# Where attention values are normalised: per unit on VectorE, or once per token tile on GpSimd

## The chip, the cores and the metric

The program runs on one core of a Trainium2 chip. The metric is the device time of one execution in microseconds (us). The engines are named as in the profile: PE is TensorE's matrix multiplication and PEld its weight load, DVE is VectorE, ACT is ScalarE, POOL is GpSimd and SP is SyncE, which here issues the DMAs.

## The reference

Four batch elements of 512 tokens by 512 channels pass through two layers. The second layer's cross-attention is where the change is:

```python
x = x + tanh(g_xattn[0]) * wkv(layernorm(x), ctx)          # a scan over the tokens
x = x + tanh(g_ffn[0])  * bitlinear_ffn(layernorm(x))      # 512 -> 2048 -> 512, int8 groups
x = x + tanh(g_xattn[1]) * attention(layernorm(x), ctx)
x = x + tanh(g_ffn[1])  * ternary_linear(layernorm(x))

# attention: 16 heads of 32 channels, queries from x, keys and values from ctx
attn = softmax(einsum('bnhd,bmhd->bhnm', q, k) * scale)
o    = einsum('bhnm,bmhd->bnhd', attn, v)
out  = qdq(o) @ qdq(wp).T + bp                             # qdq: int8, one scale per token
```

## The kernel before

A batch element `b` goes through four generators in turn: `wkv_layer`, `ffn_layer`, `attention_layer` and `ternary_layer`. Neighbouring elements overlap: while element `b` is in attention, element `b+1` is in its FFN and element `b+2` or `b+3` in its scan. Each generator is a list of small steps, and `line(gen, parts)` gives the steps a place on a common axis, measured in slots of an FFN; `run` takes them in order of place. The Tile framework's scheduler then settles the order of instructions on each engine, from that order and from what is ready, so that a change in one layer moves instructions of others. Each engine works through its own queue in order.

The attention of one element is cut into 16 units: eight pairs of heads `p`, each for two halves `h` of the tokens (two token tiles of 128). A unit goes through these steps:

- `scores` (line 948 and 950 of the kernel before): PE forms the scores `s_ps`, DVE takes the negated maximum of each row (`at_nm`), and ACT takes the exponential into `at_P`. ACT's accumulator puts the row's sum into the unit's small tile `at_sum`.
- `turned` (line 970): PE turns `at_P` into `pt_ps`, and ACT copies it to `at_PT`.
- `values` (line 990): PE multiplies by the values into `o_ps`, and ACT copies it to `at_os`, 128x128. It is unnormalised and has channels on the partitions.
- `collect` (lines 998 and 1000): PE turns it back into `ot_ps`, DVE takes the reciprocal `at_rt` of the unit's four sums, and DVE multiplies `ot_ps` by it into the unit's place in `o_all` (tile `at_o`, tokens on the partitions, one copy of it).

After the 16 units, `project_out(t)` runs for each of the four token tiles. DVE takes the largest magnitude of the 512 channels (line 222, `at_s` from `at_o`), ACT rounds (line 231), PE turns (`qr_ps`), ACT copies (line 238), PE multiplies by the output weights (`p_ps`), DVE scales (line 1036, `at_y`), and the result is added to `xb` (line 1037, on GpSimd for the first two elements). `in_steps` starts the four tiles one step after the other. The ternary layer follows: layer normalisation, `tf_xn` on GpSimd and `tf_s` on DVE.

The last element (`alone`) has no FFN beside it and takes another path through `turned` and the ending. PSUM tiles of `o_ps`, `ot_ps`, `qr_ps`, `p_ps` and others share three buffers with the tag `m`; score and FFN tiles share three with the tag `hp`.

Other names that the prediction uses: `wk_*` are tiles of the scan of the next element (its reciprocals at line 640, products at lines 632 and 645 on DVE, 630 and 635 on GpSimd). `ff_hp`, `ff_z`, `qg_*` and `hr` belong to the FFN.

Of the kernel before, what the change touches and what calls it, by code (L numbers as in the profile page):

```python
# [10 lines left out]
F32 = mybir.dt.float32  # L11
# [5 lines left out]
ALU = mybir.AluOpType  # L17
# [4 lines left out]
P = 128  # L22
# [8 lines left out]
def kernel(  # L31
# [36 lines left out]
    nc = tc.nc  # L68
    NB, T, D = x.shape
    FF = w1.shape[0]  # L70
    NT, NC, NF = T // P, D // P, FF // D
    NH, DH = 16, 32
# [8 lines left out]
    sm = ctx.enter_context(tc.tile_pool(name="small", bufs=4))  # L81
# [45 lines left out]
    def psum_tile(name, tag, dtype=F32):  # L127
        pool, bufs = psum["now"]
        return pool.tile([P, D], dtype, name=name, tag=tag, bufs=bufs[tag])

    def bank(name, dtype=F32):

        return psum_tile(name, "m", dtype)
# [13 lines left out]
    def in_turn(ins):  # L147


        if "on" in turn:  # L150
            if "ahead" in turn:
                behind(ins, turn["ahead"])
            turn["last"] = ins
        return ins
# [6 lines left out]
    def matmul(*args, **kwargs):  # L161
        return in_turn(nc.tensor.matmul(*args, **kwargs))  # L162

    def transpose(*args):
        return in_turn(nc.tensor.transpose(*args))  # L165
# [55 lines left out]
    def absmax(dst, src):  # L221
        nc.vector.tensor_reduce(dst, src, AX.X, ALU.max, apply_absolute_value=True)

    def int8_scale(s, r, amax):

        nc.vector.tensor_scalar(s, amax, 1.0 / 127.0, 1e-8, ALU.mult, ALU.max)
        nc.vector.reciprocal(r, s)

    def rounded(src, r):

        nc.scalar.activation(src, src, AF.Identity, bias=magic[:, 0:1], scale=r)

    def transposed_rows(dst, src):

        pt = bank("qr_ps")
        for c in range(NC):
            transpose(pt[:, c * P : (c + 1) * P], src[:, c * P : (c + 1) * P], ident)
        nc.scalar.activation(dst, blocks(pt), AF.Identity, bias=magic[:, 1:2])
# [599 lines left out]
    whole = {}  # L838

    def attention_layer(b, xb, pool, tiles=range(NT)):  # L840
# [5 lines left out]
        lo, n = tiles[0] * P, len(tiles) * P  # L846
        alone = b == NB - 1
        if b not in whole:
            whole[b] = (
                pool.tile([P, NC, T], BF16, name="at_xqT", tag="at_xqT", bufs=1),  # L850
                pool.tile([P, T], F32, name="at_sxb", tag="at_sxb", bufs=1),
                pool.tile([P, NT, D], F32, name="at_o", tag="at_o", bufs=1),
            )
        xqT, sxb, o_all = whole[b]

        def row(name, dtype=F32):
            return pool.tile([P, D], dtype, name=name, tag="at_row", bufs=ROWS)
# [24 lines left out]
        qR, kR, V, PT, sums, made, lanes, out_s = {}, {}, {}, {}, {}, {}, {}, {}  # L882
# [54 lines left out]
        def scores(k, i, t):  # L937

            p, h = units[k]
            if k not in sums:  # L940
                sums[k] = sm.tile([P, 2, 2], F32, name="at_sum", tag="at_sum")
            at = t * P
            sp = psum_tile("s_ps", "hp")
            matmul(
                sp, lhsT=qR[k][:, i, at : at + P], rhs=kR[p][:, i, :], start=True, stop=True
            )
            nm = sm.tile([P, 1], F32, name="at_nm", tag="at_nm", bufs=8)
            nc.vector.tensor_reduce(nm, sp, AX.X, ALU.max, negate=True)  # L948
            lanes[k, i, t] = pool.tile([P, T], F32, name="at_P", tag="at_P", bufs=6)
            nc.scalar.activation(  # L950
                lanes[k, i, t],
                sp,
                AF.Exp,
                bias=nm,
                accum_out=sums[k][:, t, i : i + 1],
            )
# [35 lines left out]
        def collect(k):  # L992

            p, h = units[k]
            pt = bank("ot_ps")[:, 0:P]
            transpose(pt, out_s.pop(k), ident)
            rt = sm.tile([P, 2, 2], F32, name="at_rt", tag="at_rt")
            nc.vector.reciprocal(rt, sums.pop(k))
            at = tiles[0] + 2 * h
            nc.vector.tensor_tensor(  # L1000
                o_all[:, at : at + 2, p * 64 : p * 64 + 64].rearrange(
                    "p t (i d) -> p t i d", d=DH
                ),
                pt.rearrange("p (i t d) -> p t i d", i=2, d=DH),
                rt.unsqueeze(3).to_broadcast([P, 2, 2, DH]),
                ALU.mult,
            )
# [9 lines left out]
        def project_out(t):  # L1017
            s = sm.tile([P, 2], F32, name="at_s", tag="at_s")
            o = o_all[:, t, :]
            absmax(s[:, 0:1], o)  # L1020
            int8_scale(s[:, 0:1], s[:, 1:2], s[:, 0:1])
            rounded(o, s[:, 1:2])
            yield True
            oqT = pool.tile([P, NC, P], BF16, name="at_oqT", tag="at_oqT")
            transposed_rows(oqT, o)
            yield True
            pp = bank("p_ps")
            for c in range(NC):
                matmul(
                    pp, lhsT=oqT[:, c, :], rhs=wpT[:, c, :], start=(c == 0), stop=(c == NC - 1)  # L1030
                )
            if b > NB - 3:
                y = wk.tile([P, D], F32, name="at_y", tag="wk_v")
            else:
                y = row("at_y")
            nc.vector.scalar_tensor_tensor(y, pp, s[:, 0:1], swp_b, ALU.mult, ALU.mult)
            (nc.vector if b > NB - 3 else nc.gpsimd).tensor_tensor(
                xb[:, t, :], xb[:, t, :], y, ALU.add
            )
            yield True  # L1040
# [9 lines left out]
        def end(ts):  # L1050

            yield from together([project_out(t) for t in ts])
            means, scale = statistics(b, xb, ts)
            yield from together([ternary(b, xb, pool, t, means, scale) for t in ts])
# [7 lines left out]
        for k in range(len(units) + 2):  # L1062
# [3 lines left out]
            for i in range(2):  # L1066
                if now:
                    scores(k, i, 0)
# [13 lines left out]
            for i in range(2):  # L1082
                if now:
                    scores(k, i, 1)
# [5 lines left out]
            if k > 1:  # L1090
                collect(k - 2)
            if now:
                p, h = units[k]
# [12 lines left out]
        if alone:  # L1106
            yield from ending
        else:
            yield from in_steps([project_out(t) for t in tiles], 1)
# [66 lines left out]
    def ternary_layer(b, xb, pool):  # L1176
        if b == NB - 2:
            r, scale = statistics(b, xb, range(NT))
            yield
        else:  # L1180
            r, scale = layernorm(xb, rms=True, pinned=False), None
        yield from in_steps([ternary(b, xb, pool, t, r, scale) for t in range(NT)], 1)
# [9 lines left out]
    def late(make):  # L1192
        yield from make()
# [26 lines left out]
    SLOTS = NT * NF + 1  # L1220

    def line(gen, *parts, aside=False):
        lines.append({"gen": gen, "parts": parts, "step": 0, "aside": aside})
# [124 lines left out]
    for b in range(NB):  # L1348
        if b:
            early = (0.99, 1.0, 4) if b == 1 else (b - 0.19, b - 0.1, 3), (b - 0.08, b, 1)  # L1350
            line(
                late(lambda b=b: ffn_layer(xs[b])),
                *((early[0],) if b == 1 else early),
                (b, b + 16 / SLOTS, 64),
                (b + 16 / SLOTS, b + 17.75 / SLOTS, 7),
            )
        start = b + 1 + 4.95 / SLOTS
        end = start + 18 / SLOTS
        line(
            late(lambda b=b: attention_layer(b, xs[b], at)),  # L1360
            (b + 1.0 if b == 0 else b + 0.7, b + 1.03 if b == 0 else b + 0.9, 5),
            (b + 1 + 1.7 / SLOTS, b + 1 + 3.7 / SLOTS, 5),
            (b + 1 + 3.75 / SLOTS, b + 1 + 4.35 / SLOTS, 2),
            (start, end, 72),
            (end, end + 2.4 / SLOTS, 6)
            if b != NB - 2
            else (end - 0.15 / SLOTS, end + 4.65 / SLOTS, 6),
            (end + 2.4 / SLOTS, end + 3.4 / SLOTS, 4),
        )
        if b < NB - 1:  # L1370
            line(
                late(lambda b=b: ternary_layer(b, xs[b], at)),
                (end + 3 / SLOTS, end + 8 / SLOTS, 8)
                if b < NB - 2
                else (end + 4.85 / SLOTS, end + 11.85 / SLOTS, 7),
                aside=b < NB - 2,
            )
# [46 lines left out]
```

## Time and profile before

| | |
|---|---|
| median of 3 runs | 1095.68 us (1094.95 to 1096.86) |
| the profiled execution's own time | 1094.21 us |
| its span, first to last instruction | 1092.4 us |
| mean granted TensorE clock | 0.956 |
| busy: PE, DVE, ACT, POOL | 86%, 76%, 67%, 29% |
| share of the chain that ended last: PE, DVE, ACT, POOL | 49%, 22%, 14%, 5% |

The span lies 1.8 us below the profiled execution's time, and the median of the runs 1.5 us above it. The shares of busy time are means over stages with different limits: while a scan runs beside attention and FFN, DVE is full; between the scans PE is.

### The profile page before, as it was taken

To read this page: it belongs to the slowest core of one execution; us is meant where nothing else is said; L and a number is where in the kernel's file an instruction comes from. 1 tells how busy PE (TensorE), PEld (TensorE's weight loads), DVE (VectorE), ACT (ScalarE), POOL (GpSimd) and SP (SyncE) were. 2 spreads that over 40 slices of the span, in tenths; PEclk is the share of its full clock that TensorE was granted. 3 is DMA by queue.
4 is the path that set the end of the run, shared out by engine and by line. 5 is a ranking of instruction groups with operands and counts; after the bars stand their busy time and mean duration, and the time that the engine had idled before them with its cause. 6 is when DMAs were issued, how large, how long until landed. Compare 5 with 4: busy or idle time off the path is not lost.

```text
span 1092.4 us, 17928 instructions
## 1 busy us (share of the span) xinstructions
PE 943.3 (86%) x6350; PEld 680.0 (62%) x6380; DVE 827.0 (76%) x1600; ACT 729.9 (67%) x1490; POOL 320.7 (29%) x328
## 2 busy tenths in 40 slices
PE   3879997998879888799997886999999999878975
PEld 2345564565557666677775665677776777655652
DVE  5985548757876899896769898966687866579976
ACT  5656755567545776667877576677685777877863
POOL 3831104423333254621215545412122410100000
PEclk8889999999999999999999798999999999989998
DMA  8188845464445674645576354655574563244311
GB/s 288 39 272 317 323 169 190 144 221 155 154 146 181 221 234 127 231 129 169 185 234 204 121 177 133 204 195 180 184 231 156 184 210 116 59 148 116 116 42 39
DMA packets 85674, 189.68 MB, mean 174 GB/s; under 512 B 12241, under 2 KB 36817, under 8 KB 74577
## 3 DMA queue, kind: packets, MB, share of 16 engines
q1 hardware_dynamic: 85584, 188.53, 51.7%
q8 instruction: 51, 0.84, 0.3%
q14 instruction: 39, 0.31, 0.1%
HBM read 148.65 MB, written 39.85 MB: 173 GB/s over the span
## 4 chain that ended last, share of the span: by engine, by line
PE 49%; DVE 22%; ACT 14%; POOL 5%; issue 5%; DMA 4%; SPq 1%; ACTq 0%; POOLq 0%; DVEq 0%
PE ff_hp L162 15%; PE pt_ps L165 7%; PE ff_acc L162 6%; PE o_ps L162 4%; PE v_ps L162 4%; PE s_ps L162 3%; ACT at_P L950 3%; DVE wk_q L640 3%; ACT at_PT L970 3%; DVE at_nm L948 2%; PE k_ps L162 2%; DVE wk_p L634 1%; PE qr_ps L165 1%; PE tp_ps L165 1%; ACT wk_e L612 1%
## 5 line engine op out<-in xcount | busy, mean ns | idle before, releaser
L162 PE MATMUL ff_hp<-wT,xp 128*128 128x512 f32 x1024 | 275.7, 412 | 6.6 <-DVE ff_z L746 3.7
L162 PEld LDWEIGHTS ff_hp<-wT,xp 128*128 128x128 f32 x1024 | 195.4, 196 | 54.6 <-DVE ff_z L746 5.7
L950 ACT ACTIVATE at_P<-s_ps,at_nm 128x512 f32<-128x512 f32 x256 | 175.0, 690 | 45.2 <-DVE at_nm L948 43.4
L948 DVE TENSOR_REDUCE at_nm<-s_ps 128x1 f32<-128x512 f32 x256 | 166.6, 677 | 38.4 <-PE s_ps L162 37.9
L970 ACT COPY at_PT<-pt_ps 128x512 f32<-128x512 f32 x224 | 131.2, 590 | 72.6 <-PE pt_ps L165 71.9
L685 POOL TENSOR_TENSOR ff_z<-qg_b,qg_s 128x512 f32<-128x512 bf16 x64 | 71.9, 1124 | 314.6 <-ACT qg_b L684 304.7
L165 PE MATMUL pt_ps<-ident,at_P 128*128 128x128 f32 x1024 | 155.4, 280 | 9.0 <-ACT at_PT L970 4.3
L165 PEld LDWEIGHTS pt_ps<-ident,at_P 128*128 128x128 f32 x1024 | 118.1, 142 | 47.3 <-ACT at_PT L970 10.9
L162 PE MATMUL ff_acc<-wT,hr 128*128 128x512 f32 x512 | 137.6, 409 | 5.2 <-DVE hr L697 2.6
L162 PE MATMUL s_ps<-at_kR,at_qR 128*128 128x512 f32 x256 | 103.0, 464 | 24.0 <-ACT at_P L950 17.6
L162 PEld LDWEIGHTS ff_acc<-wT,hr 128*128 128x128 f32 x512 | 92.9, 191 | 26.2 <-DVE hr L697 4.2
L162 PE MATMUL o_ps<-at_PT,at_V 128*32 128x128 f32 x2048 | 75.4, 281 | 4.7 <-ACT at_PT L970 2.8
L162 PEld LDWEIGHTS o_ps<-at_PT,at_V 128*32 128x32 f32 x2048 | 54.8, 111 | 28.6 <-issue 11.6
L746 DVE SCALAR_TENSOR_TENSOR ff_z<-ff_z,ff_hp 128x512 f32<-128x512 f32 x64 | 43.4, 679 | 37.0 <-ACT ff_z L745 36.9
L745 ACT ACTIVATE ff_z<-ff_hp,coef 128x512 f32<-128x512 f32 x64 | 44.1, 688 | 40.5 <-PE ff_hp L162 38.1
L750 DVE SCALAR_TENSOR_TENSOR ff_z<-ff_hp,coef,ff_z 128x512 f32<-128x512 f32 x64 | 47.7, 745 | 30.2 <-PE ff_hp L162 30.1
L684 ACT CAST qg_b<-qg_i 128x512 bf16<-128x512 int8 x80 | 49.3, 617 | 27.4 <-DVE qg_i L680 17.3
L162 PEld LDWEIGHTS s_ps<-at_kR,at_qR 128*128 128x128 f32 x256 | 43.3, 194 | 36.4 <-ACT at_P L950 25.2
L162 PE MATMUL v_ps<-wkvT,cT 128*128 128x512 f32 x128 | 60.5, 618 | 5.5 <-DVE wT L303 2.3
L162 PE MATMUL k_ps<-cT,wkvT 128*128 128x512 f32 x128 | 61.3, 631 | 2.3 <-ACT wk_k L584 1.0
L640 DVE RECIPROCAL wk_q<-wk_q 128x256 f32<-128x256 f32 x32 | 54.5, 1722 | 3.0 <-POOL wk_q L635 1.6
L696 ACT CAST hr<-tp_ps 128x512 fp32r<-128x512 f32 x64 | 37.6, 588 | 21.7 <-PE tp_ps L165 21.7
(180 smaller groups left out, 1669.4 us busy)
## 6 DMA issues: line engine op xcount, KB each, us to landing
wT<-wD SPq DMA_DIRECT2D x72, 1024.0 KB, 5.4
wn<-in_L_ffn_w_dram SPq DMA_DIRECT2D x18, 1024.0 KB, 6.2
at_kR<-kD SPq DMA_DIRECT2D x128, 128.0 KB, 4.0
at_qR<-qD SPq DMA_DIRECT2D x256, 64.0 KB, 2.5
wD<-wT SPq DMA_DIRECT2D x12, 1024.0 KB, 4.2
kD<-k_half SPq DMA_DIRECT2D x16, 512.0 KB, 2.8
qD<-at_half SPq DMA_DIRECT2D x32, 256.0 KB, 2.2
cn<-in_ctx_dram SPq DMA_DIRECT2D x8, 512.0 KB, 5.9
```

The source lines that it names most:

```text
L162: return in_turn(nc.tensor.matmul(*args, **kwargs))
L165: return in_turn(nc.tensor.transpose(*args))
L640: nc.vector.reciprocal(half, half)
L684: nc.scalar.copy(qb, qi)
L685: nc.gpsimd.tensor_tensor(grouped(src), grouped(qb), s.unsqueeze(2).to_broadcast([P, NG, GS]), ALU.mult)
L696: nc.scalar.copy(part[:, 0, :], pt)
L745: nc.scalar.activation(z, hp, AF.Tanh, scale=coef[:, 0:1])
L746: nc.vector.scalar_tensor_tensor(z, z, 1.0, hp, ALU.add, ALU.mult)
L750: nc.vector.scalar_tensor_tensor(z, hp, coef[:, 1:2], z, ALU.mult, ALU.mult)
L948: nc.vector.tensor_reduce(nm, sp, AX.X, ALU.max, negate=True)
L950: nc.scalar.activation(lanes[k, i, t], sp, AF.Exp, bias=nm, accum_out=sums[k][:, t, i : i + 1],)
L970: made[k] = nc.scalar.copy(dst, blocks(pt))
```

## The change

In the first three elements, `collect` has no arithmetic any more: ACT copies the turned, unnormalised values from PSUM into `o_all`. The sums no longer lie in a small tile for each unit but in one tile `at_all` for the element, 128 partitions by 4 token tiles by 16 heads, of which there is one copy. `project_out` begins with a new step: DVE takes 16 reciprocals for each token (one instruction for a token tile), GpSimd multiplies the token tile's 16 heads of 32 channels by them in place, and then the old first step follows. The steps of the ending rise from 6 to 7, over the same places. The last element works as before.

```diff
+                pool.tile([P, NT, NH], F32, name="at_all", tag="at_all", bufs=1),
...
             if k not in sums:
-                sums[k] = sm.tile([P, 2, 2], F32, name="at_sum", tag="at_sum")
+                if alone:
+                    sums[k] = sm.tile([P, 2, 2], F32, name="at_sum", tag="at_sum")
+                else:
+                    sums[k] = sum_all[:, 2 * h : 2 * h + 2, 2 * p : 2 * p + 2]
...
             transpose(pt, out_s.pop(k), ident)
+            if not alone:
+                nc.scalar.copy(
+                    o_all[:, 2 * h : 2 * h + 2, p * 64 : p * 64 + 64].rearrange(
+                        "p t (i d) -> p t i d", d=DH
+                    ),
+                    pt.rearrange("p (i t d) -> p t i d", i=2, d=DH),
+                )
+                return
             rt = sm.tile([P, 2, 2], F32, name="at_rt", tag="at_rt")
             nc.vector.reciprocal(rt, sums.pop(k))
...
             o = o_all[:, t, :]
+            if not alone:
+                rt = sm.tile([P, NH], F32, name="at_rt", tag="at_rt")
+                nc.vector.reciprocal(rt, sum_all[:, t, :])
+                heads = o.rearrange("p (n d) -> p n d", d=DH)
+                nc.gpsimd.tensor_tensor(
+                    heads, heads, rt.unsqueeze(2).to_broadcast([P, NH, DH]), ALU.mult
+                )
+                yield True
             absmax(s[:, 0:1], o)
...
-            (end, end + 2.4 / SLOTS, 6)
+            (end, end + 2.4 / SLOTS, 6 + (b < NB - 1))
             if b != NB - 2
-            else (end - 0.15 / SLOTS, end + 4.65 / SLOTS, 6),
+            else (end - 0.15 / SLOTS, end + 4.65 / SLOTS, 7),
```

More of the change, by code (lines that the diff above doesn't have):

```diff
@@ L852, in attention_layer @@
                 pool.tile([P, NT, D], F32, name="at_o", tag="at_o", bufs=1),
+                pool.tile([P, NT, NH], F32, name="at_all", tag="at_all", bufs=1),
             )
-        xqT, sxb, o_all = whole[b]
+        xqT, sxb, o_all, sum_all = whole[b]
         def row(name, dtype=F32):
```

## The prediction

> **What bounds the kernel now.** I read the page's first part, then busy time by stretches, then the chain of work that ended last inside the stretch that matters, then the groups by form. The page says that PE is the fullest engine and DVE the next:
>
> ```profile
> PE 943.3 (86%) x6350; PEld 680.0 (62%) x6380; DVE 827.0 (76%) x1600; ACT 729.9 (67%) x1490; POOL 320.7 (29%) x328
> ```
>
> This mean hides two regimes, which the windows show (start:end, length, busy us of PE, PEld, DVE, ACT and POOL, granted clock, DMA):
>
> ```profile
> 400.00:436.00 36.00, 31.85 (x250) 24.60 (x250) 35.57 (x55) 27.39 (x59) 16.57 (x16) 1.00 0.47 153
> 576.00:592.00 16.00, 12.17 (x62) 8.69 (x61) 16.00 (x24) 12.29 (x24) 10.01 (x8) 1.00 0.57 203
> 628.00:664.00 36.00, 26.93 (x196) 21.59 (x196) 33.89 (x68) 23.68 (x49) 18.25 (x20) 0.89 0.46 148
> 490.00:568.00 78.00, 75.38 (x606) 59.45 (x606) 53.79 (x123) 59.69 (x132) 15.41 (x16) 1.00 0.58 196
> 690.00:820.00 130.00, 126.01 (x970) 98.35 (x976) 96.13 (x221) 96.35 (x212) 28.19 (x27) 1.00 0.60 195
> ```
>
> In the first three rows a scan runs beside attention and FFN, and DVE is busy for 94 to 100% of the time. In the last two PE is busy for 97%, and DVE rests for a quarter or more. So DVE work is worth its time only in rows like the first three. The chain inside the third (start, length, what) is DVE instruction after DVE instruction, with no wait between:
>
> ```profile
> 653.64 0.68 DVE at_nm L948
> 654.32 0.66 DVE ff_z L750
> 654.98 0.60 DVE wk_e L645
> 655.58 0.60 DVE qg_s L222
> 656.17 0.20 DVE at_o L1000
> 656.37 0.08 DVE qg_s L676
> ```
>
> A product of `collect` stands in it with 0.20 us. PE meanwhile waits; the waits of PE in 570:690 (us, times, longest) begin with these:
>
> ```profile
> PE qr_ps L165 <- ACT tf_xn L231: 8.6, 1, 8.6
> PE qr_ps L165 <- ACT at_o L231: 3.9, 1, 3.9
> ```
>
> The first is the ternary layer of the first element, late because DVE is full; the second is the rounding in `project_out`, which the change puts one step later. The prices come from the groups by form:
>
> ```profile
> L1000 DVE TENSOR_TENSOR at_o<-ot_ps,at_rt 128x128 f32<-128x128 f32 x64 | 17.9, 282 | 3.0 <-PE ot_ps L165 2.8 <-PE qr_ps L165 0.2
> L990 ACT COPY at_os<-o_ps 128x128 f32<-128x128 f32 x64 | 17.1, 268 | 12.5 <-PE o_ps L162 12.5
> L632 DVE TENSOR_TENSOR wk_q<-wk_e,wk_q 128x512 f32<-128x512 f32 x16 | 16.2, 1013 | 0.2
> L678 DVE RECIPROCAL qg_r<-qg_s 128x8 f32<-128x8 f32 x80 | 15.5, 195 | 0.7
> L1037 POOL TENSOR_TENSOR xb<-xb,at_y 128x512 f32<-128x512 f32 x8 | 10.2, 1280 | 15.6 <-DVE qg_s L676 8.7 <-DVE at_s L227 3.3 <-DVE at_y L1036 2.5
> L998 DVE RECIPROCAL at_rt<-at_sum 128x4 f32<-128x4 f32 x64 | 10.0, 164 | 1.5 <-ACT at_P L950 1.5
> L1037 DVE TENSOR_TENSOR xb<-xb,at_y 128x512 f32<-128x512 f32 x8 | 5.5, 684 | 0.0
> ```
>
> **What is removed.** 48 of the 64 collects lose a reciprocal and a product on DVE: 0.164 + 0.282 = 0.446 us each, 21.4 us in all. Only part lies on the path. By the start times of line 1000, three collects (400.8, 416.8, 426.4) lie in the first stretch: 3 x 0.446 = 1.3 us. Five (576.8, 616.6, 630.1, 641.1, 656.1) lie between 576 and 664, where DVE's lateness becomes PE's wait of 8.6 us: 2.2 us. In the other stretches up to 980 the chain's own pieces of lines 998 and 1000 add up to 1.5 us, and I take those alone. What is late next when DVE is faster is PE, which is busy 75 to 88% in the first three stretches, so there is room. Gain: 1.3 + 2.2 + 1.5 = 5.0 us. It cannot be below 1.5; the upper end would be all 13 collects outside the stretches full of PE, 5.8 us, and what a shorter PE wait gives back in clock.
>
> **What is added on DVE.** Twelve reciprocals of 128x16. The rows for 4 and 8 columns are 0.164 and 0.195 us, so I take 0.2 each. Only the first element's four fall near a full DVE: 4 x 0.2 = 0.8 us. In the built order of the changed kernel each stands behind the row maxima of the last units, so it waits for an exponential on ACT; the 64 old reciprocals waited for that 1.5 us in all, so I add nothing (at worst one exponential each, 0.7 us, with FFN gates queued behind it).
>
> **What is added on ACT.** 48 copies of 128x128 out of PSUM. Line 990 is the same form: 0.268 us, 12.9 us in all. In the built order the copy stands between the last `at_PT` copy (0.590 us) and the FFN's `hr` copy, which waits for PE 21.7 us over 64 anyway; PE's `ot_ps` comes directly after the `pt_ps` that this `at_PT` copy reads, so the copy finds its data there. Behind it in the queue wait `hr` and the next exponentials. Line 990 is on the chain with 0.27, 0.15 and 0.03 us between 380 and 980, and I charge the same to the new copies: 0.5 us. Bounds: 0, and ACT's 14% share of the chain, 1.8 us.
>
> **What is added on GpSimd.** Twelve products of 128x512. Line 1037 is nearest (two f32 inputs, in place): 1.28 us, 15.4 us in all, on an engine that is 29% busy. The first maximum of an ending now has a reciprocal and one or two products ahead of it. In the built order DVE has an FFN product and two row maxima before it (0.7 + 2 x 0.68 = 2.0 us behind `hr`) against 2 x 1.28 = 2.6 us of products that start before `hr` (0.6 us): covered. On PE a group of scores and eight FFN matmuls now stands ahead of the first `qr_ps`, which covers the later step; if that cover fails, the wait of 3.9 us grows by the product. The four products of the first ending run while DVE is full. DVE's products of two SBUF tiles there take 1.013 us (line 632, GpSimd busy beside it) and 0.684 us with GpSimd idle (line 1037 on DVE): 0.33 us for a meeting, and I charge four, 1.3 us. Bounds: 0, and the rival below.
>
> The Trainium skill, "SBUF — State Buffer", section "Who interferes with whom", speaks against the change here: a DVE instruction with two SBUF inputs and a GpSimd instruction that reads SBUF exclude each other for the whole instruction. The trace agrees as far as line 632 goes, whose slowest took 1.78 us. By that rule as the worst case, an estimate from the page and line 1037, each of twelve products would hold DVE for 1.28 us and the change would lose some 12 us.
>
> **Waits that it makes.** With one copy of `at_all`, the first exponential of the next element must wait for the last reciprocal of this one. The built order puts that reciprocal 18 DVE instructions ahead of the row maximum which the exponential needs anyway: nothing. The steps' places keep their ends. No DMA is moved.
>
> **The sum.** -5.0 + 0.8 + 0.5 + 1.3 = -2.4 us against the profiled execution: 1094.2 - 2.4 = 1091.8. The median lies 1.5 us above that execution, so I predict 1093.3 us. About 0.2%, 2.2 us, is what a measurement can tell from no change; the forecast is just outside it. With the bounds of its terms it reaches from 1090.5 to 1095.
>
> **The rivals.** *DVE's time counts more than its own length.* After PE's waits the granted clock is low: 0.74 in 616:628, where PE is busy for 11.9 of 12 us, and 0.90 in 664:676. If the waits before fall away, so do 12 x 0.26 = 3.1 and 12 x 0.10 = 1.2 us, 4.3 more: 1089. For it: the chain there is nearly all DVE. Against it: GpSimd's scan products stand in the same chain.
>
> *Nothing.* In the full stretches ACT takes over as DVE is relieved, 13 copies x 0.268 = 3.5 us against 5.0 gained, and the terms cancel: 1095.5. For it: ACT's exponentials follow DVE's maxima in the chain; against it: ACT is busy only 66 to 77% there.
>
> *Slower: the product at the endings.* GpSimd's queue holds the products in front of FFN rescalings and scan products, and everything in `project_out` waits for them. GpSimd is 63% busy in 576:592. If cover fails at all three endings, each loses the reciprocal and two products, 0.2 + 2 x 1.28 = 2.8 us, 8.3 in all; with only the first stretch's 1.3 us gained that is +7: 1102.5. It decides as soon as less than half of a pair of products is hidden.
>
> **How the numbers follow.** The forecast has 0.39, a quarter of it within 0.2%; the larger gain 0.17; nothing 0.13; the slower case 0.31. Faster: 0.29 + 0.17 = 0.46. Same: 0.10 + 0.13 = 0.23. Slower: 0.31. The range from 1087 to 1102.5 leaves out half of the slower case and some of the larger gain, about 0.2.
>
> **What would show it.** Lines 998 and 1000 must remain with 16 each, DVE's busy time fall by about 19 us, ACT's rise by 13 and POOL's by 15. DVE should have less than 34 us in the counterpart of 628:664 and PE's wait on `tf_xn` should shrink. I am wrong if DVE's maxima of `at_o` wait for GpSimd by more than 1.3 us in all, if PE's wait for the rounding grows, or if the copies on ACT take more than 0.3 us because they wait for `ot_ps`.

## The result and the profile after

The change made the kernel slower. The changed kernel ran at 1099.13 us (median of 15 runs, 1096.74 to 1105.75), the kernel before beside it at 1095.59 us (15 runs, 1093.10 to 1097.84). The ratio is 1.0038, with a 95% interval of 1.0028 to 1.0048, or 4.2 us. The profiled execution of the changed kernel took 1097.93 us with a span of 1096.2 us and a granted clock of 0.960.

The page's busy line of the changed kernel, then three of the windows that were shown of before:

```profile
PE 939.6 (86%) x6348; PEld 679.6 (62%) x6380; DVE 820.5 (75%) x1516; ACT 736.4 (67%) x1538; POOL 336.8 (31%) x340
```

```profile
400.00:436.00 36.00, 32.31 (x254) 25.31 (x254) 34.00 (x55) 28.70 (x63) 18.11 (x18) 1.00 0.50 156
...
628.00:664.00 36.00, 27.95 (x225) 22.25 (x225) 31.52 (x62) 23.05 (x50) 22.14 (x23) 0.91 0.50 163
490.00:568.00 78.00, 74.61 (x600) 58.46 (x600) 52.29 (x109) 59.43 (x138) 16.25 (x17) 1.00 0.58 196
```

ACT gained 6.5 us and POOL 16.1, but DVE lost only 6.5 us where 19 were forecast. In 628:664 DVE went from 33.89 to 31.52 us, so that stretch did become lighter. The groups by form of what was added (busy, mean ns | idle of the engine before them, and for what):

```profile
L1002 ACT COPY at_o<-ot_ps 128x128 f32<-128x128 f32 x48 | 13.4, 278 | 0.7 <-PE ot_ps L165 0.7
L1036 POOL TENSOR_TENSOR at_o<-at_o,at_rt 128x512 f32<-128x512 f32 x12 | 12.8, 1088 | 49.8 <-ACT at_o L1002 44.1 <-DVE at_rt L1034 5.6
...
L1034 DVE RECIPROCAL at_rt<-at_all 128x16 f32<-128x16 f32 x12 | 3.0, 247 | 4.8 <-ACT at_P L954 4.8
```

Every duration is close to its forecast (0.268, 1.28 and 0.2 us). So the loss is not in the length of the new instructions. PE's waits in 570:690, where the gain was expected, begin with:

```profile
PE qr_ps L165 <- ACT tf_xn L231: 6.0, 1, 6.0
PE qr_ps L165 <- ACT at_PT L974: 3.6, 2, 2.7
```

The wait for the rounding of `at_o` (3.9 us before) is gone, and a new one for `at_PT` has come. Aligning the two traces by the end of each unit's `at_os` copy gives the losses a place: the changed kernel is 2.3 us behind at unit 15, is 3.4 us ahead by unit 27, and is 5.0 us behind at unit 53 of 64. So a gain at element 0's ending is outweighed by losses behind it, most of them in stretches where units are worked off and 2.6 us of them in element 2's ending. The gain and the losses both need a cause.

### The profile page after: what moved, and what is told of

Same layout as the page of the kernel before. It is cut to its first block, busy times and chain, and to the rows that moved or that the text cites. A ratio compares the mean times of both kernels' runs of the same rounds, so it can differ in the third digit from the quotient of the medians.

```text
span 1096.2 us, 17917 instructions
## 1 busy us (share of the span) xinstructions
PE 939.6 (86%) x6348; PEld 679.6 (62%) x6380; DVE 820.5 (75%) x1516; ACT 736.4 (67%) x1538; POOL 336.8 (31%) x340
## 4 chain that ended last, share of the span: by engine, by line
PE 46%; DVE 23%; ACT 13%; POOL 7%; issue 5%; DMA 5%; SPq 0%; ACTq 0%; POOLq 0%; DVEq 0%
PE ff_hp L162 14%; PE pt_ps L165 6%; PE ff_acc L162 6%; PE v_ps L162 4%; PE o_ps L162 4%; ACT at_P L954 3%; PE s_ps L162 3%; DVE wk_q L640 3%; DVE at_nm L952 3%; PE k_ps L162 2%; ACT at_PT L974 2%; ACT wk_e L612 2%; PE tp_ps L165 2%; DVE wk_p L634 1%; DVE ff_z L750 1%
## 5 line engine op out<-in xcount | busy, mean ns | idle before, releaser
L954 ACT ACTIVATION_READ_ACCUMULATOR at_P<-s_ps,at_nm 128x1 f32 x256 | 52.5, 205 | 0.0
```

The source lines that it names most:

```text
L954: nc.scalar.activation(lanes[k, i, t], sp, AF.Exp, bias=nm, accum_out=sums[k][:, t, i : i + 1],)
```

## The experiments

A difference in per cent of the kernel before, times 1095 us, gives the us named below. Each ratio comes from five to twelve executions beside the kernel before on the same chip, with its 95% interval. A unit is one of the sixteen parts of an element's attention, numbered through the kernel from 0 to 63, and an element's ending is its `project_out`.

**One element at a time, and the extra step alone.** In the first three kernels `alone` became a test for one element (and the planner's 7 went with it):

```diff
-            if not alone:
+            if b in MOVED:          # (0,), (1,) or (2,)
```

> The change in element 0 alone; elements 1 to 3 keep reciprocal and normalising read on VectorE, with the plan of before. Theory A, each element pays and earns in its own stretch: element 0's ending is the one place where VectorE is full (33.89 us of 36 busy before), and the aligned traces lost 7 us there after a rise of 2.3; so about 4 us less than before, 1091.5, and VectorE's busy time in 628:664 falls by 2. Theory B, the product's way over GpSimd costs more than the lighter read brings wherever it stands: 1096.5 to 1097. Theory C, the time is set by the order in which the scheduler puts the neighbouring work and not by the moved operations: anything from 1092 to 1099, and the sum of the three one-element differences is not the 3.5 us of the whole.

> The change in element 1 alone. Theory A: element 1's ending gave about 1 us back, and the ternary stage of element 1 that follows it lost 3.8 us between 864 and 877; so 2.5 us more than before, 1098, with TensorE waiting for the stored probabilities (L974) behind a late rounding (L231) in the counterpart of 864:877. Theory B: 1096.5 to 1097. Theory C: the loss of 3.8 us is there only if VectorE's maximum of the third token tile (L222) stands ahead of the second tile's scale, whatever the element that was changed.

> The change in element 2 alone, whose ending lies beside element 3's own normalising. Theory A: the aligned traces lost 3 to 4 us there (units 45 to 53, where the collecting copy, product, maximum and rounding follow one another and element 3's exponentials stand behind the rounding): 1099. Theory B: 1096.5 to 1097. Theory C: anything from 1093 to 1099.

The fourth is the kernel before with nothing but the extra step:

```diff
             o = o_all[:, t, :]
+            if not alone:
+                yield True
             absmax(s[:, 0:1], o)
...
-            (end, end + 2.4 / SLOTS, 6)
+            (end, end + 2.4 / SLOTS, 6 + (b < NB - 1))
             if b != NB - 2
-            else (end - 0.15 / SLOTS, end + 4.65 / SLOTS, 6),
+            else (end - 0.15 / SLOTS, end + 4.65 / SLOTS, 7),
```

> The kernel before, with only the extra step of each token tile's ending (a bare yield ahead of the maximum in elements 0 to 2) and the planner's 7 in place of 6; no operation is moved, added or taken away. Theory A, the operations are what costs: no change, 1095.0 to 1096.2. Theory C, the order decides: the steps alone shift the endings of elements 0 to 2 against the feed-forward work, and the time moves by 1.5 us or more either way.

Element 0 alone: 1091.02 us, ratio 0.9973 (0.9961 to 0.9984). Element 1: 1093.47, 0.9991 (0.9982 to 1.0000). Element 2: 1095.39, 1.0009 (1.0000 to 1.0019). Theory A has element 0's time right but not its reason: VectorE's busy time in 628:664 was 33.36 us, 0.5 below before and not 2. It misses elements 1 and 2. The three differences sum to -0.27%, while the whole change is +0.38%: the parts do not add.

The extra step alone ran at 1085.54 us, ratio 0.9924 (0.9909 to 0.9939). That is 8.3 us less than before without any operation moved. From unit 15 to unit 20, in element 0's ending, the kernel before takes 99.8 us, the step alone 92.9 and the whole change 93.4. The gain that the change has there is the step's (without the step, below, the change takes 98.9). PE's waits in 570:690 with the step alone begin with these, and neither the rounding of `at_o` (3.9) nor `at_y` (2.7) is left:

```profile
PE qr_ps L165 <- ACT tf_xn L231: 9.0, 1, 9.0
PE s_ps L162 <- ACT at_P L950: 3.9, 3, 2.1
```

The order of instructions on PE shows why. The wait of 3.9 us stood at the ending's third token tile, and 32 products with the values `o_ps`, the turned tile behind them and eight FFN products stood behind it in PE's queue (timeline of PE: start, length, line, operation, with the wait in brackets):

```profile
599.47 1.11 PE L165 MATMUL qr_ps<-ident,at_o 128*128 128x128 f32 x4 [3.87 <-ACT at_o L231]
...
602.23 1.94 PE L162 MATMUL o_ps<-at_PT,at_V 128*32 128x128 f32 x32
604.09 1.11 PE L165 MATMUL pt_ps<-ident,at_P 128*128 128x128 f32 x4
```

With the step this work stands ahead of the same `qr_ps`, which then does not wait:

```profile
597.48 1.08 PE L162 MATMUL o_ps<-at_PT,at_V 128*32 128x128 f32 x32
599.23 0.66 PE L165 MATMUL pt_ps<-ident,at_P 128*128 128x128 f32 x4 [0.67 <-DVE at_s L226]
599.64 2.10 PE L162 MATMUL ff_acc<-wT,hr 128*128 128x512 f32 x8
601.58 0.60 PE L165 MATMUL qr_ps<-ident,at_o 128*128 128x128 f32 x4
```

The shorter waits are only half of it. From unit 0 to unit 54 the profiled executions before and with the step differ by 9.3 us (616.9 and 607.6). PE's idle time fell by 4.3 us, and its busy time with the same products by 5.0 (554.0 to 549.0), at a mean granted clock of 0.967 before and 0.980 with the step.

So the question turned round. Against the step alone, the whole change costs 1.14% more, 12.5 us (some 13.5 by the two medians, which the expectations below use). Which of its operations?

**The operations one by one.** The kernel `no_product` leaves the normalising out: its product covers one element per partition.

```diff
 no_product:         heads[:, 0:1, 0:1], heads[:, 0:1, 0:1], rt[:, 0:1].unsqueeze(2), ALU.mult
 steps_and_product:  step alone, and  nc.gpsimd.tensor_tensor(heads, heads, ones[:, 0:NH]..., ALU.mult)
 copy_on_vector:     nc.scalar.copy(o_all...)          ->  nc.vector.tensor_copy(o_all...)
 product_on_vector:  nc.gpsimd.tensor_tensor(heads...) ->  nc.vector.tensor_tensor(heads...)
```

> The whole change with the per-tile product cut down to one element per partition, so that the normalising is left out and the collecting copies, the reciprocals and the extra step stay. The extra step alone ran at 1085.5 and the whole change at 1099.1: 13.5 us lie between them, and the aligned traces put 9.3 of these into the stretches in which units are worked off and 4.2 into the endings. Theory A, the collecting copy on ScalarE holds up the loop of scores, exponential and transposed probabilities in every unit, and the product costs only in the endings: 1094 to 1096. Theory B, the product on GpSimd and the order around it cost nearly all: 1086 to 1088. Theory C, the 13.5 us are one new order against another and no operation's price: it can land anywhere between 1085 and 1099, and the parts will not add up.

> The kernel before with the extra step, which ran at 1085.5, and a product of the already normalised rows by a tile of ones on GpSimd ahead of that step, at the place and in the size of the change's product; reciprocals and normalising read stay per unit on VectorE. It shows the price of the product alone. Theory A: its 4.2 us in the endings, 1089 to 1090. Theory B: 1097 or more. Theory C: no sum rule with the run without the product (the two differences to 1085.5 do not add to 13.5).

> The whole change, but the collecting copy runs on VectorE instead of ScalarE. Theory A: the 9.3 us of the unit stretches come back, 1089 to 1091, and TensorE's wait for the stored probabilities (L974) between 385 and 571, 2.6 us in the changed kernel, falls back to about 0.7. Theory B: no better than the change, 1098 to 1100. Theory C: no ordered answer.

> The whole change, but the product runs on VectorE (a 128x512 product of two operands took 0.68 to 0.80 us there before, 12 of them 9 us) instead of GpSimd (1.09 us each). Theory A: the endings lose the trip to GpSimd (1.05 to 1.5 us a product) and add 0.7 us each to a full VectorE: within 2 us of the change, 1097 to 1101. Theory B: if GpSimd's share and the order around it cost nearly all of the 13.5 us, well below the change, 1090 to 1093.

Without the product: 1090.09 us, 0.9963 (0.9951 to 0.9976). Step and product: 1087.62, 0.9938 (0.9924 to 0.9952). Copy on VectorE: 1088.59, 0.9943 (0.9931 to 0.9956). Product on VectorE: 1099.00, 1.0039 (1.0026 to 1.0053).

The product by itself costs 0.14%, 1.5 us over the step alone, which the two intervals (0.9924 to 0.9952 and 0.9909 to 0.9939) do not tell from nothing, and in the whole change VectorE or GpSimd doing it makes no difference (1.0039 and 1.0038). The collecting copy is what matters: taking it from ScalarE to VectorE brings 10.4 us of the 12.5 back (0.95%), although VectorE is the fuller engine (75% busy against 67%). In the profiled executions 5.1 us of them lie in units 11 to 12 and 36 to 37, which the order of the neighbours decides (below). But without the product the change is at 0.9963, 4.3 us over the step, not 12.5, so the two do not add either (theory C has a part in it).

**Without the step, with copies only, and two pins.** A pin, `behind(x, y)`, makes the scheduler place x after y on its engine.

```diff
 no_extra_step:   the change without  yield True  behind the product, and with 6 steps again
 steps_and_copy:  step alone, and
+                spare = sm.tile([P, P], F32, name="at_spare", tag="at_spare", bufs=1)
+                nc.scalar.copy(spare, pt)          # then reciprocal and product as before
 pin_scale:       behind(<row maximum of tf_xn>, <last scale operation of the tile before>)
 pin_addition:    behind(<xb += bp_b>, <last FFN rescaling on GpSimd>)
```

> The whole change without its extra step: copies, reciprocals and products stay, the bare yield behind the product goes and the planner counts 6 again. The extra step alone took 9 us off the kernel before, at its three endings. Theory D, the step and the moved operations are separate and opposite effects (step -9, operations +12.5): 1106 to 1109. Theory E, the step works only where the normalising read is on VectorE, or the product already parts the rounding from the maximum as the step does: 1098 to 1101. The forecast's reading, the operations themselves relieve VectorE in element 0's ending: units 15 to 20 still take 6 us less than before.

> The kernel before with the extra step, and in elements 0 to 2 one more copy of each unit's turned values on ScalarE into a tile that nobody reads; reciprocals and the normalising read stay on VectorE and do the work. 48 copies of 0.28 us are 13.4 us of ScalarE. Theory A, the copies hold up ScalarE's other work (stored probabilities, exponentials) in the unit stretches: 4 to 6 us over the 1085.5 of the step alone, with the additions of the projection's constant (L875 in the changed kernel) standing ahead of the rescaling of the feed-forward tile again at units 11 to 12 and 27 to 28. Theory F, it is not the copies but what is no longer on VectorE or the product: within 1 us of 1085.5.

> The whole change, and in the ternary stage each token tile's maximum (L222) is held behind the last small operation of the tile before, which is their order in the kernel before. Theory C for this one place: the 3.8 us between units 36 and 37 go, 1095 to 1096, and ScalarE's wait of 1.8 us for that scale too. Theory A, ScalarE's load is the cause and the order only shows where it comes out: less than 1.5 us.

> The whole change, and the additions of the projection's constant to the rows on GpSimd (1.28 us each) are held behind the rescaling of the feed-forward tile that the program issues before them. Theory C for this place: the 2.0 us of units 11 to 12 and the 1.0 us of 27 to 28 go, 1096 to 1096.5. It moves these additions further back than in the kernel before, so that it may shift other work on GpSimd; if the two stretches come back and the time does not, something later took it.

No extra step: 1100.26 us, 1.0061 (1.0044 to 1.0077). Step and copies: 1098.23, 1.0042 (1.0026 to 1.0058). Pinned scale: 1095.00, 1.0011 (1.0001 to 1.0021). Pinned addition: 1095.15, 1.0014 (1.0002 to 1.0025).

Inside the change the step is worth 2.5 us and not 8.3 (theory E). It still takes 5.8 us off between units 15 and 16, but 2.6 come back in element 2's ending and 2.3 between units 36 and 37. The 48 copies alone, with VectorE's work all still there, cost 1.18%, 12.9 us over the step. That is more than theory A expected, and it rejects theory F.

Both pins missed their target. Units 36 to 37 stayed 3.4 us longer (3.8 without the pin), units 11 to 12 stayed 2.0 us longer. The first one failed in an instructive way. The pin put the second tile's small operations in their old order, and one of them then met GpSimd's product (timeline: start, length):

```profile
863.42 1.29 POOL L1167 TENSOR_TENSOR tf_xn<-tf_xn,gamma_b 128x512 f32<-128x512 f32 x1
863.50 1.23 DVE L1183 TENSOR_TENSOR tf_s<-tf_s,coef 128x1 f32<-128x1 f32 x1
```

One element per partition took 1.23 us, and ended 0.02 us after GpSimd. Of the 16 times that this operation runs there, it took 0.13 to 0.15 us in the 13 that no GpSimd instruction overlapped; the other two (0.30 us, one tile earlier, and 0.23) also ended 0.02 us after the GpSimd instruction beside them. So the rounding behind it was as late as without the pin. Both pinned kernels gained about 0.25% elsewhere; where from was not settled.

**Load or order.** The scheduler had given the neighbouring work a new order in every one of these kernels. The next kernels take that freedom away. After the program is recorded, the instructions that two kernels share are tied behind their predecessors in the other kernel's order, on VectorE, ScalarE, GpSimd and TensorE. The copies, the products and all of `collect`'s reciprocals and reads on VectorE are placed freely.

```diff
+    made = {i.name: i for i in nc.all_instructions()}
+    for names in ORDER:                     # one list for each engine
+        for one, two in zip(names, names[1:]):
+            tc.add_manual_dep(made[two], one, DependencyInfo(NoSync, DATA))
```

> The whole change, with every other instruction of VectorE, ScalarE, GpSimd and TensorE held in the order of the kernel with the extra step alone (1085.5); only the copies, reciprocals and products of the change are placed freely between them. Theory O, the 13.5 us between the two are the new order of the neighbouring work: 1083 to 1088. Theory L, they are the load of the moved operations themselves on ScalarE and GpSimd: 1095 to 1099.

> The mirror of the run above: the kernel with the extra step alone (no operation moved, reciprocal and normalising read on VectorE), with every other instruction held in the order of the changed kernel. Theory O: the changed kernel's time or more, since VectorE has its reads back, 1097 to 1105. Theory L: 1084 to 1088.

> The change without its extra step, and every other instruction held in the order of the kernel before: this is the change as the forecast priced it, the operations moved and nothing else. The forecast's sum was 2.4 us less than before, 1092 to 1094 on this chip. Theory L: 3 to 10 us more than before.

> The kernel with the extra step and the 48 added copies on ScalarE that nobody reads, which ran at 1098.2, with every other instruction held in the order of the step alone. The copies' own load of 13.4 us of ScalarE stays. Theory O: 1085 to 1088. Theory L: 1096 to 1099.

The change in the step's order: 1095.72 us, 1.0012 (1.0000 to 1.0024). The step in the change's order: 1093.99, 0.9985 (0.9969 to 1.0002). The moved operations in the old order: 1100.06, 1.0044 (1.0032 to 1.0056). The copies in the step's order: 1098.78, 1.0031 (1.0020 to 1.0042). Theories O and L each have a part: of the 12.5 us (1.14%) the order makes 2.8 or 6.7, the operations 9.6 or 5.8, depending on which is put in first; each of these differences is uncertain by about 2 us. The aligned traces tell the two apart by place. The table has us beyond the step alone, from one unit's `at_os` to another's, from the profiled executions:

| units | before | change | change, step's order | step, change's order | copies, step's order | copies without bank |
|---|---|---|---|---|---|---|
| 0 to 11 | 0.1 | -0.6 | 1.5 | 0.4 | 4.0 | 0.2 |
| 11 to 12 | 0.0 | 2.0 | 0.1 | 1.8 | 0.1 | 0.1 |
| 12 to 15 | 0.0 | -0.3 | 1.6 | -0.8 | 0.7 | -0.1 |
| 15 to 20, ending 0 | 6.9 | 0.5 | 1.5 | -0.5 | 1.5 | 0.1 |
| 20 to 31 | 0.1 | 2.4 | 4.6 | 2.1 | 3.9 | 0.2 |
| 31 to 36, ending 1 | 2.7 | 1.5 | 0.0 | 1.6 | 1.1 | 0.0 |
| 36 to 37 | 0.0 | 3.8 | 0.0 | 4.3 | 0.0 | 0.0 |
| 37 to 46 | 0.0 | 1.4 | 1.0 | 2.0 | 2.7 | 2.0 |
| 46 to 54, ending 2 | -0.4 | 2.2 | 1.2 | -0.5 | -0.2 | 1.1 |

Units 11 to 12 and 36 to 37 are pure order: they go when the order goes and come when it comes, with no operation moved. At unit 11 it is a row maximum that waits for GpSimd and now stands ahead of the FFN's product on VectorE. First the step alone, then the step in the change's order (timeline, with the wait in brackets):

```profile
526.63 0.69 DVE L746 SCALAR_TENSOR_TENSOR ff_z<-ff_z,ff_hp 128x512 f32<-128x512 f32 x1 [0.52 <-ACT ff_z L745]
528.00 0.69 DVE L222 TENSOR_REDUCE at_s<-at_xn 128x1 f32<-128x512 f32 x1 [0.68 <-POOL at_xn L219]
```

```profile
527.22 0.69 DVE L222 TENSOR_REDUCE at_s<-at_xn 128x1 f32<-128x512 f32 x1 [1.65 <-POOL at_xn L219]
527.82 0.68 DVE L746 SCALAR_TENSOR_TENSOR ff_z<-ff_z,ff_hp 128x512 f32<-128x512 f32 x1
```

With the pin on GpSimd's addition the row maximum still stood ahead of that product, so it was at the wrong engine. Units 20 to 31 are of both kinds: they lose 4.6 us with the operations in the step's order, and 2.1 us by the order with no operation moved.

**What the copy costs, with the order fixed.** The first passage of the step alone, in which a tile is turned and collected:

```profile
401.04 0.27 PE L165 MATMUL ot_ps<-ident,at_os 128*128 128x128 f32 x1
...
401.47 0.28 DVE L1000 TENSOR_TENSOR at_o<-ot_ps,at_rt 128x128 f32<-128x128 f32 x1
...
401.81 0.66 PE L165 MATMUL tp_ps<-ident,ff_xn 128*128 128x128 f32 x4
```

The same passage of the changed kernel:

```profile
402.65 0.27 PE L165 MATMUL ot_ps<-ident,at_os 128*128 128x128 f32 x1
...
404.21 0.66 PE L165 MATMUL tp_ps<-ident,ff_xn 128*128 128x128 f32 x4 [0.85 <-ACT at_PT L974]
...
405.74 0.26 ACT L1002 COPY at_o<-ot_ps 128x128 f32<-128x128 f32 x1
```

`pt_ps`, `ot_ps` and `tp_ps` take turns in the three buffers `m`. VectorE reads `ot_ps` 0.16 us after it is ready, and the next `tp_ps` goes into its bank. ScalarE comes to it 2.8 us later, after scan work, an `at_PT` copy and an FFN copy; all three banks are full, and PE waits for the first of them, which an `at_PT` copy sets free. The copy takes 0.26 us, but the bank is held for 3.1. From the end of each `ot_ps` to the end of its last reader, over the first three elements, the mean is 1.12 us before and with the step alone, 1.59 in the changed kernel, 2.22 with the added copies; 8, 8, 16 and 23 of the 48 take over 2 us. With the collecting copy on VectorE, the run that gave 10.4 us back, it is 1.12 again, and 7 take over 2 us.

The last test keeps the copies and their places in ScalarE's queue, and lets them read another tile, so that they hold no bank:

```diff
-                nc.scalar.copy(spare, pt)            # turned rows, PSUM
+                nc.scalar.copy(spare, turned)        # the rows before they are turned, SBUF
```

> The kernel of the run before with the 48 added copies in the order of the step alone (1098.8; the step alone 1085.5), where each copy reads the unit's rows before they are turned (at_os, in SBUF) instead of the turned rows in PSUM. Copies, their number and size, and the place of every instruction in its queue on all four engines stay the same; what goes is that ScalarE's copy holds the PSUM bank of the transposition. In the step alone that bank was held 1.12 us on the mean after the transposition and 2.22 us with the copies. Theory L, ScalarE's time is what costs: 1096 to 1099. Theory P, the bank that is kept until ScalarE comes to its copy is what costs, since TensorE's next transposition needs one of three: 1086 to 1090.

> The extra step alone, given to element 3 as well (the planner counts 7 there too); no operation is moved. In elements 0 and 1 the step took 6.8 and 2.7 us off the endings, in element 2 it added 1.9. If it parts a wait of TensorE in element 3's ending too: 1083 to 1085; if there is no such wait at the end: within 1 us of 1085.5; if it lengthens the last chain by one step of the planner: 1087 to 1090.

Copies without the bank: 1088.72 us, 0.9952 (0.9937 to 0.9967). From 1.0031 to 0.9952 is 8.6 us; what stays above the step alone, 0.28% or 3.1 us, is ScalarE's time for 48 copies of 0.30 us. Each is uncertain by about 2 us. The time lies where theory P put it, and the 8.6 us are three quarters of the 11.7 us that the copies cost in the step's order. The table's last column is zero up to unit 37, where the three us of ScalarE's own time begin. PE's waits for `at_PT` in 395:1000 at transpositions that do not read it, and so wait for its bank, first of the change, then of the copies with the bank, then without it:

```profile
PE tp_ps L165 <- ACT at_PT L974: 7.2, 8, 1.6
...
PE qr_ps L165 <- ACT at_PT L974: 5.4, 3, 2.7
```

```profile
PE qr_ps L165 <- ACT at_PT L970: 5.5, 3, 2.7
PE tp_ps L165 <- ACT at_PT L970: 5.1, 6, 1.6
```

```profile
PE qr_ps L165 <- ACT at_PT L970: 2.2, 2, 1.3
PE tp_ps L165 <- ACT at_PT L970: 1.6, 3, 0.7
```

12.6 and 10.6 us against 3.8. With the moved operations in the old order they are 9.2 (5.7 and 3.5), before 4.3 (2.1 and 2.2). PE's other waits change too, so this is no sum of the 8.6 us: from unit 0 to unit 54 the copies with the bank take 10.2 us longer than without it, of which PE's idle time makes 5.3 and its busy time 4.9, at a mean granted clock of 0.970 and 0.975.

Three things go with the bank in this test. VectorE's read of `ot_ps` stood behind ScalarE's four times, 4.3 us in all. ScalarE waited twice for the transposition before its copy, 3.1 us in all. And 33 of VectorE's 48 reads stand 1 to 8 instructions later in its queue than without the bank. The aligned traces speak against the two kinds of waits: the two executions lie 3.8 us apart at unit 4, before any of the six, and around each of the six the distance grows by at most 0.6 us. The later reads keep the bank longer as well, and what they cost apart from that was not tested. In the change itself VectorE does not read the tile, so the bank's share is only a remainder: with the order fixed the operations cost 9.6 us over the step, of which 3.1 is the price of ScalarE's time and 1.5 that of the product, each measured in another kernel; some 5 us are left for the bank.

The step in element 3 too: 1085.13 us, 0.9920 (0.9905 to 0.9935), the same as without it within the intervals. The fastest version measured is thus the kernel before with the extra step, at 0.992 of the time before.

## Why the prediction was wrong

The time lies in the range, at the slower case's side; the direction was wrong. None of the three signs of being wrong that the prediction named came: the row maxima of `at_o` waited 0.9 us for GpSimd, PE's wait for the rounding fell from 5.2 us in the whole execution to 1.3, and the copies took 0.278 us. The signs watched how long the new instructions take and wait, and not what waits for them. Step by step:

The moved operations in the old order leave PE's waits in 570:690, from which the gain should have come, as they were before (8.6 and 3.9 us):

```profile
PE qr_ps L165 <- ACT tf_xn L231: 8.5, 1, 8.5
PE qr_ps L165 <- ACT at_o L231: 3.9, 1, 3.9
```

- **The gain of 5.0 us on VectorE did not show.** It is the first step that failed, in the order of the sum. With the operations moved and the order kept, PE's wait that it was to shorten stays, as the lines above show, and units 15 to 20 took 100.0 us there and 99.8 before. In the changed kernel that wait did shrink to 6.0 us, but with the neighbours in the step's order it is 9.0. A part of the gain may lie hidden under the copies, which cost 1.5 us in these units in the step's order; it was not measured alone. The size was wrong too. The records of short instructions overlap their neighbours': of the 21.3 us that the 96 removed instructions add up to, VectorE ran nothing else for 8.4 us, and counted from the end of the instruction before they took 13.7 us, 0.285 us a collect and not 0.446. The chain that the prediction showed had said so, with 0.20 us for the product. And some of what stayed became longer (the FFN's `qg_i` products by 2.1 us in sum). Busy time fell by 6.5 us.
- **The copies at 0.5 us, at most 1.8, were the second and larger failure.** 48 such copies cost 11.7 us in the step's order, and 3.1 us when they hold no bank. Length (0.278 us) and own wait (0.7 us) were as forecast. The forecast asked how long the copy waits for the bank, and not how long the bank waits for the copy. It had named the queue behind the copy, not the work ahead of it. `collect` shares its three banks with PE's other transpositions.
- **The extra step at nothing was the third.** The forecast read the group of scores and FFN products ahead of `qr_ps` as cover for the product. It was a gain: 8.3 us alone, 2.5 inside the change. The 3.9 us wait for the rounding stood in a fence of the prediction, one sentence away.
- **The order of the neighbours was not in the sum.** It was used as given by the built order at the places that the change touches; its price was 1.9 us without the step (1.0044 to 1.0061, with intervals that overlap) and 2.8 with it.
- **GpSimd's product had the right number by luck**: forecast 1.3 us, measured 1.5, which is within the noise of nothing. The forecast placed it in element 0's ending. In the kernel with the step and the product that ending, units 15 to 20, took 1.5 us less than with the step alone, and units 20 to 31 took 2.2 us more. (The 1.013 us of line 632 was also read too simply: four of its sixteen met no GpSimd instruction, and the twelve that did took 1.12 us.) The slower rival, cover failing at all endings, had the right sign by the wrong mechanism: the product on VectorE changes nothing (1.0039).
- The reciprocals took 0.247 us and waited 4.8 us for exponentials, where the forecast had 0.2 and nothing.
- The first rival had named the granted clock after PE's waits, and the sum left it out. In the two pairs of kernels above it came with about half of each difference.

The account closes like this, by differences of which each is uncertain by about 2 us: before, +4.8 us for the moved operations in the old order, +1.9 for the new order, -2.5 for the step, +4.2 in all. The forecast had -2.4 for the first and nothing for the rest.

The Trainium skill, "PSUM — Partial Sum Buffer", section "Summary: rules for kernel authors", says to empty PSUM promptly, for want of room. The runs agree and put a number on whom it hits: a 0.26 us copy that came 2.8 us late stood beside a wait of 0.85 us at one of PE's next transpositions, where the step alone has none. "SBUF — State Buffer", section "Who interferes with whom", says that a VectorE instruction with two SBUF inputs and a GpSimd instruction that reads SBUF exclude each other for the instruction. The 1.23 us for one element per partition agrees with it: it ended 0.02 us after GpSimd's instruction.

## What to carry to other kernels

When a read of PSUM moves to another engine, price how long that engine's queue keeps the bank, not how long the copy takes, and look who allocates next from the same buffers: the less busy engine can be the later one. Take a step that only changes the order out of an edit and measure it by itself; here it was worth more than the edit, and it made a loss look like a gain at one place. Where a scheduler reorders neighbours, tie the shared instructions to one order before a difference is called the price of an operation.

## What the runs showed that was not expected

- An empty step in a planner's list was worth 0.76% (8.3 us); at element 0's ending it put 44 matrix products ahead of the one that had waited 3.9 us in PE's queue.
- Less waiting on PE came with a higher granted clock: of 9.3 us between two kernels with the same products on PE, 4.3 were its idle time and 5.0 its busy time (clock 0.967 and 0.980).
- The same instructions with and without a new order of the work around them differ by 1.9 to 6.7 us, as much as the change itself (4.2), and one-element variants do not add up (-0.27% against +0.38%).
- Two engines that read the same PSUM tile were not independent: in the built program VectorE's read waited four times for ScalarE's, up to 1.5 us.
- A product of 128x1 took 1.23 us beside a GpSimd product of 1.29 us, and 0.13 to 0.15 us with no GpSimd instruction beside it.
